# A ranked graph pass in two float32r terms of full width instead of three bf16 terms of half width

## The chip, the core and the metric

The kernel runs on one core of a Trainium2 chip. The core has a matmul engine (TensorE: PE for the matmuls, PEld for its weight loads), VectorE (DVE), ScalarE (ACT), GpSimd (POOL) and SyncE (SP, which issues most DMAs). Each engine works through its own queue in order. SBUF is the working memory; PSUM, eight banks of 128 partitions by 512 float32 numbers, takes the matmul results. The metric is the device time of one execution in microseconds; the median of runs is compared.

## What is computed

Four graph layers over x (3327 nodes by 64 features) and a sparse weighted adjacency matrix, padded here to 3328 by 3328. Every layer is a layernorm and a relu, then the layer's own work, added to x. Layer 0 is two gated cells (GRU), each with one product adj @ (h W). Layer 2 is three products with adj * adj, layer 3 two products with adj. Layer 1 is the one that matters here:

```python
support = input @ weight
mask = (adj != 0).astype(support.dtype)
rank = jnp.cumsum(mask, axis=1)
deg = rank[:, -1:]
k = jnp.minimum(deg, float(MAX_NEIGH))        # 100
pos = rank - (deg - k)
w = mask * jnp.where(pos > 0, DECAY ** (k - pos), 0.0)   # DECAY = 0.5
out = w @ support + bias
```

So the last neighbour of a row has weight 1, the one before it a half, and so on: every weight is an exact power of two that depends on how many neighbours stand behind it. There are eight passes over the adjacency matrix, k = 0 to 7; k = 2 is this "ranked" pass, k = 3, 4, 5 use the squared matrix, the rest the plain one.

## The kernel before

The transposed matrix lies in HBM. A `Tile` is 128 sources (q = 0 to 25) by the two halves of the targets, for one of two groups of target columns: group 0 is chunks 0 and 1 (384 columns each for either half), group 1 is chunks 2 (384) and 3 (512). A unit is (pass k, chunk c, tile t). For every plain or squared unit `propagate` (L579) runs two f32 matmuls, one for each half of the targets; their 64 stationary columns stand in the two halves of the array, so that the two results share one PSUM bank.

`joint(g, k, ...)` (L655) lists the units of two successive passes of one group, with one load of each tile for both: `joint(0, 1)` is k=1 and k=2 of group 0, `joint(1, 2)` is k=2 and k=3 of group 1. The second pass of a pair lags by `later` tiles. `run` (L711) goes through the list of units: it loads tiles ahead into NBUF = 20 buffers, has masks and squares made ahead, calls `expand` (L484) EXPAND = 3 units ahead, and then `propagate`. That order, written out when the program is built, is the order of every engine's queue. Work between passes (`after_1`, `after_2`, ...) runs as tasks: `spend` counts model time, and when a task's time is up its next instructions are put in the queues.

In the ranked pass a tile's 0/1 mask (bf16, made by DVE at L466; its row 127 is replaced by the counts of neighbours behind this tile, by a POOL DMA at L471) is multiplied by the triangular matrix `tri`. Its entries are multiples of 2^7, so the sum in PSUM is 128 times an exponent, and where no edge is, far below zero. ACT (L523, Relu with a bias) or DVE (L521, add and max with 0) turns that sum into an int16, whose bits are those of the bf16 number 2^exponent: `e`. Which engine takes the half s=1 is set by a rule on tile and chunk (L511 to L519); s=0 is always ACT. The features of the pass are split by `in_three` (L912) into three bf16 terms, which add up to the f32 value. A ranked unit is thus, on PE, two triangle products (L510, L307, each a pair of half-width matmuls) and three terms (L607, each a pair). A `SPECIAL` unit at the end of each chunk handles the sources in row 127 of all tiles, with weights `lastw` (L576) and features `lasty` (gathered by POOL DMAs, L928).

PSUM is split in two pools of four banks: sums, and temporaries, though `take` (L316) lends a sums bank when it has been free for longer. After the pass, `after_2` (L961) evacuates the sum, multiplies by the weight matrix (block-diagonal `bd`, two targets halves at once), adds it to x and runs the next layernorm.

Of the kernel before, what the change touches and what calls it, by code (L numbers as in the profile page):

```python
# [11 lines left out]
I16 = mybir.dt.int16  # L12
AF = mybir.ActivationFunctionType
# [31 lines left out]
N, D = 3327, 64  # L45
# [14 lines left out]
TWO27 = float(2 ** 27)  # L60
CAP = 100.0
BITS = (CAP - 128.0) * TWO7

# [10 lines left out]
NBUF = 20  # L74
# [3 lines left out]
EXPAND = 3  # L78
# [5 lines left out]
def chunk_of(b):  # L84
    return next(c for c, (b0, b1) in enumerate(CH[:NC]) if b0 <= b < b1)
# [6 lines left out]
def upper(n):  # L92
    return slice(n * D, (n + 1) * D)
# [3 lines left out]
def kernel(  # L97
# [13 lines left out]
    work = ctx.enter_context(tc.tile_pool(name="work", bufs=4))  # L111
    psum = ctx.enter_context(tc.tile_pool(name="psum", bufs=1, space=bass.MemoryType.PSUM))
# [15 lines left out]
    both = [const.tile([P, 2, (b1 - b0) * P], F32, name=f"both{c}") for c, (b0, b1) in enumerate(CH[:NC])]  # L128
    both += [both[1][:, :, (CH[c][0] - CH[1][0]) * P:(CH[c][1] - CH[1][0]) * P] for c in PARTS]
# [7 lines left out]
    bitsb = const.tile([P, 1], F32, name="bitsb")  # L137
# [4 lines left out]
    lasty = const.tile([P, 2, 3, D], BF16, name="lasty")  # L142
# [95 lines left out]
    def more_constants():  # L238
# [19 lines left out]
        nc.gpsimd.memset(bitsb, BITS)  # L258
        nc.gpsimd.memset(lasty, 0.0)
# [23 lines left out]
        for h in range(2):  # L283
            nc.sync.dma_start(out=bd[upper(h), :, upper(h)], in_=weights[:, WL1:WL3])
            for i in range(2):
                nc.sync.dma_start(out=w3[upper(h), :, i], in_=weights[:, WL3 + (h + i) % 2:NW:2])
# [23 lines left out]
    idle_sums, idle_temps = deque(range(4)), deque(range(4, 8))  # L310
    banks = [psum.tile([P, CWM], F32, name=f"sum{i}") for i in range(4)]
    banks += [psum.tile([P, CWM], F32, name=f"temp{i}") for i in range(4)]

    released = [0] * 8

    def take(sums=False, either=True):  # L316


        either = either and not sums
        pool = idle_sums if sums else idle_temps  # L320
        if either and idle_sums and (not pool or released[idle_sums[0]] < released[pool[0]]):
            pool = idle_sums
        for c in list(tasks):
            if not pool and c not in running:
                advance(c)
        i = pool.popleft()
        return i, banks[i]

    def give(i):
        released[i] = max(released) + 1  # L330
        (idle_sums if i < 4 else idle_temps).append(i)
# [106 lines left out]
    def square(sq, v, turn):  # L438
        if turn % 3 or any(ch in tasks or (2, ch) in sums for ch in range(NC)):
            nc.scalar.activation(sq, v, AF.Square)  # L440
        else:
            nc.vector.tensor_tensor(sq, v, v, ALU.mult)  # L442
# [40 lines left out]

    def expand(k, c, t):  # L484

        if k == COUNT:
            return None
        w = width(c)
        if t is SPECIAL:
            g = c // 2  # L490
            w0 = (CH[c][0] - CH[GROUPS[g][0]][0]) * P
            finish(NC + 1 + g)
            return lastw[g][:, w0:w0 + w].bitcast(BF16)
        if KIND[k] == PLAIN or (KIND[k] == SQUARED and t.in_place):
            return t.view(c)
        if KIND[k] == SQUARED:
            room = Mask(t.w)
            wide = room.view.rearrange("p s w -> p (s w)").bitcast(F32)[:, :2 * w].rearrange("p (s w) -> p s w", s=2)
            square(wide, t.view(c), t.q + c)
            squared[k, c, t] = room  # L500
            return wide
        wide = work.tile([P, 2, CWM], I16, name="e", bufs=4)[:, :, :w]

        mask_pieces(t=t)
        for s in range(2):
            i, ps = take()
            mm(ps[:, :w], tri, t.mask.view[:, s, t.cols(c)])  # L510
            own = chunk_of(t.q % NB) in GROUPS[t.g]  # L511
            busy = any((k - 1, ch) in sums for ch in GROUPS[t.g])
            if t.g == 1 and not own and not relief["squares"]:

                on_vector = s and c == GROUPS[1][1]
            elif relief["pieces"]:
                on_vector = s and (t.q + c) % 4
            else:
                on_vector = s and (own if t.g == 0 and (own or busy) else c == GROUPS[t.g][1] or t.g == 1 and not own)  # L519
            if on_vector:  # L520
                nc.vector.tensor_scalar(wide[:, s], ps[:, :w], BITS, 0.0, op0=ALU.add, op1=ALU.max)  # L521
            else:
                nc.scalar.activation(wide[:, s], ps[:, :w], AF.Relu, bias=bitsb)  # L523
            give(i)
        spend(STREAM_US * w / CWM * 0.5)
        if c == GROUPS[t.g][1]:
            t.mask.free()
        return wide.bitcast(BF16)
# [4 lines left out]
    def count(t, first, last):  # L533
# [3 lines left out]
        for c in GROUPS[t.g]:  # L537
            w = width(c)
            if first:
                counts[c] = take(either=False)  # L540
# [17 lines left out]
    def last_sources(g):  # L558
# [17 lines left out]
        nc.scalar.activation(lastw[g], v, AF.Relu, bias=bitsb)  # L576
        room.free()

    def propagate(k, c, t, rhs, first, last):  # L579
# [4 lines left out]
        if first:  # L584
            sums[k, c] = [take(sums=True) for _ in range(2 if k == 7 and c == PARTS[1] else 1)]
            sums[k, c] = [sums[k, c][0], sums[k, c][-1]]
        acc = sums[k, c]
        if t is SPECIAL:
# [3 lines left out]
            terms = [[lasty[:, h, i, :] for h in range(2)] for i in range(3)]  # L592
            rhs = [rhs, rhs]
        else:
# [4 lines left out]
            terms = [[yk[:, b - CH[cs][0], s, :]] * 2 for yk in (y[k][cs] if KIND[k] == RANKED else [y[k][cs]])]  # L599
            rhs = [rhs[:, h, :] for h in range(2)]  # L600
            if KIND[k] != RANKED:
                t.used()
            if (k, c, t) in squared:
                squared.pop((k, c, t)).free()
        for n, yq in enumerate(terms):
            for h in range(2):
                nc.tensor.matmul(acc[h][1][h * D:(h + 1) * D, :w], yq[h], rhs[h], start=first and n == 0,  # L607
                                 stop=last and n == len(terms) - 1)
        if t is not SPECIAL and t.early and t.mask is None:
            make_mask(t, RANKED)  # L610
        spend(STREAM_US * w / CWM * (0.75 if KIND[k] == RANKED else 1.0))
# [300 lines left out]
    def in_three(h, c):  # L912

        room = both[c].bitcast(BF16).rearrange("p s w -> p (s w)")[:, :blocks(c) * 2 * 3 * D]
        room = room.rearrange("p (b s i d) -> p b s i d", s=2, i=3, d=D)
        terms = [room[:, :, :, i, :] for i in range(3)]
        for i in range(2):
            yield 0.8
            nc.scalar.copy(terms[i], h)
            yield 0.8  # L920
            nc.vector.tensor_tensor(terms[2] if i else h, h, terms[i], ALU.subtract)

# [6 lines left out]
        return terms  # L929
# [18 lines left out]
    def after_1(c, acc):  # L948
# [7 lines left out]
        yield from layernorm_relu(yk, c, TWO27, 1.2 * pace, squares_on_scalar=c in GROUPS[1])  # L956
        y[2][c] = yield from in_three(yk, c)
# [3 lines left out]
    def after_2(c, acc):  # L961
        m = evacuate(acc, c)
        yield 1.4
        v = dense_to_nodes(m, WL1, c)
# [23 lines left out]
    def after_5(c, acc):  # L988
# [8 lines left out]
        yield 8.0  # L997
        yield from transpose_on_vector(yk, c)
# [28 lines left out]
    joint(1, 0, sweep=6, later=4, keep=3, lag=2)  # L1027
# [58 lines left out]
```

## Time and profile before

| what | us |
| --- | --- |
| median of 3 runs | 707.11 (706.21 to 707.22) |
| span of the profiled execution, first to last instruction | 703.7 |
| DVE busy, whole span | 350.1 |
| ACT busy, whole span | 271.8 |
| f32 matmuls of the plain and squared passes (L607), busy | 534.5 |
| bf16 matmuls of the ranked terms (L607), busy | 78.5 |
| triangle matmuls (L307) into the pool of temporaries, busy | 56.8 |
| Relu to int16 on ACT (L523), 145 instructions | 66.0 and 16.6 |
| add and max on DVE (L521), 63 instructions | 38.0 |

The first exponent conversion starts at 204.5 us and the last ranked matmul ends about 338 us. Busy time of PE counts overlapping matmuls once. A group in the profile is a source line with an engine and an operation; L307 is a helper (`mm`) that several callers share.

### The profile page before, as it was taken

The page shows a single profiled execution, that of the slowest core. Times are in us where ns is not written, and L with a number is a line of the kernel's source. Part 1 is how long each engine was busy: PE and PEld are TensorE (multiplying, and loading weights), DVE is VectorE, ACT ScalarE, POOL GpSimd, SP SyncE. Part 2 cuts the span into 40 slices and gives each one's busy share as a digit, 9 for nine tenths or more (in the row PEclk, how much of TensorE's full clock was granted, in tenths as well). Part 3 has the DMA queues.
Part 4 walks back from the last instruction along what each step waited for, and adds up shares of the span by engine and source line. Part 5 has one row for each costly group of instructions (what it writes and reads, how often), then busy time and mean ns, then how long its engine had stood idle before and what let it go on. Part 6 is the DMA issues. An engine that isn't in the chain of part 4 may idle for free.

```text
span 703.7 us, 12628 instructions
## 1 busy us (share of the span) xinstructions
PE 679.8 (97%) x5100; PEld 372.9 (53%) x5100; DVE 350.1 (50%) x746; ACT 271.8 (39%) x422; POOL 80.0 (11%) x114
## 2 busy tenths in 40 slices
PE   1999999999999999999999999999999999999997
PEld 1454666643556787677444444333344444344586
DVE  7556835643997889847523105425271565005101
ACT  1014100122146888888998206832166600000101
POOL 4300000002284233111100000000000000000000
PEclk9999999999999999999999999999999999999999
DMA  9999996089686952683799649973998399927991
GB/s 344 401 385 404 406 405 241 2 314 398 209 279 253 371 177 76 246 297 96 265 390 343 245 151 409 405 276 100 398 366 271 107 391 406 406 81 276 402 403 45
DMA packets 68549, 201.31 MB, mean 286 GB/s; under 512 B 7228, under 2 KB 8228, under 8 KB 68492
## 3 DMA queue, kind: packets, MB, share of 16 engines
q1 hardware_dynamic: 65596, 199.46, 75.9%
q8 instruction: 40, 0.66, 0.4%
q10 hardware_dynamic: 720, 0.85, 0.3%
q0 software_dynamic: 2176, 0.20, 0.2%
q14 instruction: 17, 0.14, 0.1%
HBM read 199.45 MB, written 0.85 MB: 285 GB/s over the span
## 4 chain that ended last, share of the span: by engine, by line
PE 91%; DVE 7%; issue 0%; ACT 0%; DMA 0%; POOL 0%; ACTq 0%; DVEq 0%; POOLq 0%
PE sum L607 77%; PE temp L307 5%; PE temp L542 2%; PE temp L876 2%; PE sum L307 1%; DVE adj L466 1%; PE temp L774 1%; PE sum L876 1%; DVE e L521 1%; DVE st L842 1%; DVE adj L901 1%; DVE t L836 1%; DVE y L841 0%; DVE st L834 0%; DMA xs<-in_x 0%
## 5 line engine op out<-in xcount | busy, mean ns | idle before, releaser
L607 PE MATMUL sum<-adj,y 128*64 128x384 f32 (+3 forms) x3016 | 534.5, 502 | 0.7 <-DVE y L849 0.6
L607 PEld LDWEIGHTS sum<-adj,y 128*64 128x64 f32 x3016 | 243.5, 137 | 237.3 <-issue 212.4
L440 ACT ACTIVATE adj<-adj 128x768 f32<-128x768 f32 (+1 forms) x176 | 144.2, 893 | 45.8 <-PE sum L607 21.9
L466 DVE TENSOR_SCALAR adj<-adj 128x768 bf16<-128x768 f32 (+3 forms) x208 | 114.0, 597 | 39.8 <-PE temp L542 31.8
L824 ACT COPY both<-sum 64x384 f32<-64x384 f32 (+3 forms) x17 | 8.1, 478 | 192.6 <-PE sum L607 191.4
L607 PE MATMUL sum<-e,both 128*64 128x384 bf16 (+1 forms) x624 | 78.5, 339 | 0.5 <-DVE e L521 0.5
L523 ACT ACTIVATE e<-temp,bitsb 128x384 int16<-128x384 f32 (+1 forms) x117 | 66.0, 605 | 15.1 <-PE temp L307 9.9
L825 DVE COPY both<-sum 64x384 f32<-64x384 f32 (+3 forms) x17 | 9.6, 569 | 110.5 <-ACT both L824 110.5
L307 PE MATMUL temp<-adj,tri 128*64 128x384 bf16 (+1 forms) x332 | 56.8, 341 | 0.5 <-DVE e L521 0.2
L442 DVE TENSOR_TENSOR adj<-adj 128x768 f32<-128x768 f32 (+1 forms) x32 | 30.6, 1005 | 52.1 <-DMA adj<-in_adjT 33.4
L845 POOL TENSOR_TENSOR st<-st,mhalf 128x6 f32<-128x6 f32 (+1 forms) x16 | 24.0, 1498 | 283.2 <-DVE st L843 279.5
L607 PEld LDWEIGHTS <-both 128*64 128x64 bf16 x624 | 46.6, 110 | 15.5 <-issue 2.2
L307 PEld LDWEIGHTS <-tri 128*64 128x64 bf16 x416 | 33.5, 110 | 15.3 <-issue 7.1
L521 DVE TENSOR_SCALAR e<-temp 128x384 int16<-128x384 f32 (+1 forms) x49 | 30.1, 617 | 21.1 <-ACT e L523 10.5
L471 POOL DMA_DIRECT2D adj<-totals x52 | 31.5, 607 | 51.2 <-PE temp L307 40.9
L803 DVE STREAM_TRANSPOSE both<-y 32x96 f32<-32x96 f32 (+1 forms) x128 | 35.6, 278 | 2.9
L542 PE MATMUL temp<-adj,behind 128*64 128x384 bf16 x208 | 30.3, 339 | 0.9 <-DVE adj L466 0.7
L819 DVE STREAM_TRANSPOSE y<-t 32x96 f32<-32x96 f32 (+1 forms) x64 | 17.8, 278 | 24.9 <-ACT t L810 24.0
L542 PEld LDWEIGHTS <-behind 128*64 128x64 bf16 x208 | 17.0, 110 | 17.6 <-issue 15.9
L755 DVE COPY t<-sum 128x384 f32<-128x384 f32 x6 | 3.3, 555 | 35.3 <-PE sum L607 35.3
L564 POOL MEMSET adj<- 128x768 f32 (+1 forms) x2 | 1.9, 950 | 145.3 <-PE sum L607 145.3
L523 ACT ACTIVATE e<-sum,bitsb 128x384 int16<-128x384 f32 (+1 forms) x28 | 16.6, 598 | 2.5 <-PE sum L307 2.1
(132 smaller groups left out, 327.8 us busy)
## 6 DMA issues: line engine op xcount, KB each, us to landing
adj<-in_adjT SPq DMA_DIRECT2D x130, 768.0 KB, 8.5
adj<-in_adjT SPq DMA_DIRECT2D x104, 896.0 KB, 12.3
xs<-in_x SPq DMA_DIRECT2D x1, 640.0 KB
adj<-totals POOLq DMA_DIRECT2D x26, 3.0 KB, 5.1
adj<-totals POOLq DMA_DIRECT2D x26, 3.5 KB, 3.0
out<-xs ACTq DMA_DIRECT2D x2, 192.0 KB
out<-xs ACTq DMA_DIRECT2D x1, 256.0 KB
stage<-in_weights SPq DMA_DIRECT2D x2, 112.0 KB, 13.1
```

The lines of the kernel that those rows point to most:

```text
L307: nc.tensor.matmul(out[hs], lhsT[:, hs], rhs, start=start, stop=stop)
L440: nc.scalar.activation(sq, v, AF.Square)
L442: nc.vector.tensor_tensor(sq, v, v, ALU.mult)
L466: nc.vector.tensor_scalar(t.mask.view[:rows, half], t.view()[:rows, half], 0.0, None, op0=ALU.not_equal)
L471: nc.gpsimd.dma_start(out=t.mask.view[P - 1:P], in_=totals[t.g][t.q:t.q + D + 1:D, :])
L521: nc.vector.tensor_scalar(wide[:, s], ps[:, :w], BITS, 0.0, op0=ALU.add, op1=ALU.max)
L523: nc.scalar.activation(wide[:, s], ps[:, :w], AF.Relu, bias=bitsb)
L542: nc.tensor.matmul(counts[c][1][s * D:(s + 1) * D, :w], behind[:, NQ - 1 - t.q:NQ - 1 - t.q + D], t.mask.view[:, s, t.cols(c)], start=firs ...
L607: nc.tensor.matmul(acc[h][1][h * D:(h + 1) * D, :w], yq[h], rhs[h], start=first and n == 0, stop=last and n == len(terms) - 1)
L803: nc.vector.transpose(to[at:at + 32, :, q], h[q * 32:(q + 1) * 32, :, s, f * 32:(f + 1) * 32])
L845: nc.gpsimd.tensor_tensor(st[:, 3, :n], st[:, 2, :n], mhalf[:, :n], ALU.pow)
L876: nc.tensor.matmul(ps[upper(1 - s), :w], cells[:, cell, s, g, :], both[c][:, s], start=True, stop=True)
```

## The change

- The features are split in two float32r terms (`in_two`): ACT's copy rounds to float32r, DVE's subtraction gives the rest. The two stand side by side as 128 stationary columns. Each target half needs a bank of its own, so a ranked sum holds two banks for each chunk, and one matmul for each half replaces three pairs. `after_2` evacuates two banks and adds the two terms' rows by way of the weight matrix, which for this layer stands twice one above the other.
- The weights `e` are float32r. ACT computes exp(ln2/128 * sum + bias), which rounds to the exact power of two when it is written. On DVE the conversion to int16 stays, and a second instruction multiplies the bits, read as bf16, by a constant and writes float32r. The rule is now: half s=1 of a group 0 tile goes to DVE if the chunk is 1 or q is odd, all else goes to ACT. The special unit gets one such multiplication.
- The triangle product is one matmul of 128 stationary columns for each half.
- While ranked sums are open, three of four squares of k=3 go to DVE; before, all went to ACT then.
- One pool of eight PSUM banks; NBUF 19 instead of 20, EXPAND 2 instead of 3, keep=2 instead of 3 in `joint(1, 0)`. `both` buffers come from a pool and are allocated anew for the terms and again after pass 5. The scale is 2^38 instead of 2^27.

```diff
-NBUF = 20
+NBUF = 19
-EXPAND = 3
+EXPAND = 2
...
-    idle_sums, idle_temps = deque(range(4)), deque(range(4, 8))
...
+    idle = deque(range(8))
+    banks = [psum.tile([P, CWM], F32, name=f"bank{i}") for i in range(8)]
...
     def square(sq, v, turn):
-        if turn % 3 or any(ch in tasks or (2, ch) in sums for ch in range(NC)):
+        ranked = any((2, ch) in sums for ch in range(NC))
+        if turn % 4 == 0 if ranked else turn % 3 or any(ch in tasks for ch in range(NC)):
             nc.scalar.activation(sq, v, AF.Square)
...
+    def weight():
+        return work.tile([P, CWM], F32R, name="e", bufs=2 * (EXPAND + 1))
+
     def expand(k, c, t):
...
-            return lastw[g][:, w0:w0 + w].bitcast(BF16)
+            e = weight()
+            nc.vector.tensor_scalar(e[:, :w], lastw[g][:, w0:w0 + w].bitcast(BF16), DROP, None, op0=ALU.mult)
+            return e, e
...
         for s in range(2):
             i, ps = take()
-            mm(ps[:, :w], tri, t.mask.view[:, s, t.cols(c)])
...
+            nc.tensor.matmul(ps[:, :w], tri, t.mask.view[:, s, t.cols(c)], start=True, stop=True)
+            e = weight()
+            if s and t.g == 0 and (c == GROUPS[0][1] or t.q % 2):
+                bits = work.tile([P, CWM], I16, name="bits", bufs=2)
+                nc.vector.tensor_scalar(bits[:, :w], ps[:, :w], BITS, 0.0, op0=ALU.add, op1=ALU.max)
+                nc.vector.tensor_scalar(e[:, :w], bits[:, :w].bitcast(BF16), DROP, None, op0=ALU.mult)
             else:
-                on_vector = s and (own if t.g == 0 and (own or busy) else c == GROUPS[t.g][1] or t.g == 1 and not own)
...
-                nc.scalar.activation(wide[:, s], ps[:, :w], AF.Relu, bias=bitsb)
+                nc.scalar.activation(e[:, :w], ps[:, :w], AF.Exp, bias=bitsb[:, 1:2], scale=LN2 / TWO7)
             give(i)
...
-            sums[k, c] = [take(sums=True) for _ in range(2 if k == 7 and c == PARTS[1] else 1)]
+            sums[k, c] = [take() for _ in range(2 if KIND[k] == RANKED or k == 7 and c == PARTS[1] else 1)]
...
+        if KIND[k] == RANKED:
+            for h in range(2):
+                nc.tensor.matmul(acc[h][1][:, :w], terms[h], rhs[h][:, :w], start=first, stop=last)
...
-        spend(STREAM_US * w / CWM * (0.75 if KIND[k] == RANKED else 1.0))
+        spend(STREAM_US * w / CWM * (0.5 if KIND[k] == RANKED else 1.0))
...
+    def in_two(h, c):
+
+        room = stacked.tile([P, blocks(c), 2, P], F32R, name=f"both{c}")
+        yield 0.8
+        nc.scalar.copy(room[:, :, :, :D], h)
+        yield 0.8
+        nc.vector.tensor_tensor(room[:, :, :, D:], h, room[:, :, :, :D].bitcast(F32), ALU.subtract)
+        yield 1.5
...
     def after_2(c, acc):
-        m = evacuate(acc, c)
+        w = width(c)
+        m = [work.tile([P, CWM], F32, name="t2")[:, :w] for _ in range(2)]
+        nc.scalar.copy(m[0], acc[0][1][:, :w])
+        nc.vector.tensor_copy(m[1], acc[1][1][:, :w])
+        for n in range(2):
+            give(acc[n][0])
         yield 1.4
-        v = dense_to_nodes(m, WL1, c)
+        i, ps = take()
+        v = i, view(ps, c)
+        for b in range(blocks(c)):
+            for s in range(2):
+                for n in range(2):
+                    nc.tensor.matmul(v[1][upper(n), b, upper(s)], m[s][:, b * P + n * D:b * P + (n + 1) * D],
+                                     bd[:, 0, upper(0)], start=True, stop=True)
...
-    joint(1, 0, sweep=6, later=4, keep=3, lag=2)
+    joint(1, 0, sweep=6, later=4, keep=2, lag=2)
```

## The prediction

> **What bounds the kernel now.** First the page's header, its engine line and its chain of work:
>
> ```profile
> span 703.7 us, 12628 instructions
> PE 679.8 (97%) x5100; PEld 372.9 (53%) x5100; DVE 350.1 (50%) x746; ACT 271.8 (39%) x422; POOL 80.0 (11%) x114
> PE 91%; DVE 7%; issue 0%; ACT 0%; DMA 0%; POOL 0%; ACTq 0%; DVEq 0%; POOLq 0%
> ```
>
> The matmul engine (PE) ends the program, but the averages hide stages. The change touches one stage, the ranked pass, so next comes the table of engine busy time by stretch: 200 to 219 us (two ranked tiles among f32 units), 219 to 248 (group 0 against group 1's sources, beside the GRU and layernorm of group 0), 248 to 269.3 (group 0 against its own sources), and group 1 in the last three:
>
> ```profile
> 200.00:219.00 19.00, 19.00 (x144) 10.90 (x142) 16.95 (x32) 10.47 (x20) 17.80 (x20) 1.00 0.58 195
> 219.00:248.00 29.00, 27.48 (x333) 20.27 (x331) 24.19 (x52) 22.91 (x48) 5.84 (x9) 1.00 0.98 374
> 248.00:269.30 21.30, 21.30 (x267) 18.41 (x264) 18.57 (x37) 15.98 (x31) 4.94 (x9) 1.00 0.40 132
> 269.30:284.50 15.20, 13.98 (x147) 9.77 (x145) 14.91 (x30) 13.24 (x24) 6.80 (x9) 1.00 0.37 121
> 284.50:316.50 32.00, 32.00 (x256) 22.79 (x254) 19.43 (x35) 27.66 (x42) 3.76 (x7) 1.00 0.80 279
> 316.50:338.00 21.50, 21.50 (x235) 15.92 (x233) 16.14 (x29) 19.18 (x33) 3.27 (x6) 1.00 0.43 134
> ```
>
> Columns: stretch, length, then busy PE, PEld, DVE, ACT, POOL, the clock (full), DMA. PE is full nearly everywhere, but VectorE (DVE) is at 24.2 of 29.0, 18.6 of 21.3 and 14.9 of 15.2, and ScalarE (ACT) at 16 to 28 just behind. There is little room on either. Third, the timeline of one ranked unit (a chunk times a source tile) in the steady part:
>
> ```profile
> 250.09 0.36 PE L307 MATMUL temp<-adj,tri 128*64 128x384 bf16 x2
> 250.25 0.36 PE L307 MATMUL sum<-adj,tri 128*64 128x384 bf16 x2
> 250.41 0.68 PE L607 MATMUL sum<-e,both 128*64 128x384 bf16 x6
> 250.53 0.58 ACT L523 ACTIVATE e<-temp,bitsb 128x384 int16<-128x384 f32 x1 [0.23 <-DVE e L521]
> 250.70 0.56 DVE L521 TENSOR_SCALAR e<-sum 128x384 int16<-128x384 f32 x1 [0.26 <-PE sum L307]
> ```
>
> Five pairs of half-width matmuls, each pair 0.1625 us from start to start (250.09, 250.25, 250.41): 0.81 us a unit at 384 columns. At 512 columns the pairs stand 0.215 apart (269.10 to 269.32): 1.08.
>
> Last, the groups kept apart by shape, for prices:
>
> ```profile
> L523 ACT ACTIVATE e<-temp,bitsb 128x384 int16<-128x384 f32 x94 | 50.6, 585 | 13.5 <-PE temp L307 9.2 <-ACT adj L440 3.1 <-DVE e L521 0.9
> L521 DVE TENSOR_SCALAR e<-temp 128x384 int16<-128x384 f32 x26 | 14.3, 554 | 5.1 <-PE temp L307 2.6 <-ACT adj L440 1.2 <-issue 0.6
> L466 DVE TENSOR_SCALAR adj<-adj 128x768 bf16<-128x768 f32 x52 | 27.8, 582 | 16.0 <-PE temp L542 15.9
> L881 ACT ACT_TABLE_LOAD x1 | 1.3, 1283 | 0.0
> ```
>
> Queued back to back, ACT starts L523 every 0.467 us (235.29, 235.75, 236.21) and its 512-wide form every 0.575 (0.69 less the same overlap).
>
> **Matmuls.** Triangle: two full-width matmuls instead of two half-width pairs, the same streaming time. Feature terms: two full-width float32r matmuls instead of three bf16 pairs. No row shows float32r or a 128-column weight load. The nearest rows are the bf16 pair (0.1625 us at 384 columns) and the f32 pair (0.644: five units from 199.60 to 202.82). Less than the bf16 row is excluded, since as many columns stream. I take the bf16 row: the new matmul is one record over the moving tile if it is a single pass, as bf16 is, while the f32 rows hold two records a matmul. Then a unit takes four pair times instead of five: 78 units of 384 columns, 26 of 512 and the four special units (three and one) save 81 x 0.1625 + 27 x 0.215 = 19 us of PE work. At two pair times a matmul a unit takes six, and the change costs 19 us; at the f32 row, four each, it takes ten: +95. Weight loads are hidden now (64 columns 110 ns, behind 162); 128 columns at twice that, 220 ns, would expose 58 ns on each of 4 x 104 matmuls, 24 us. I take zero, since loads of the next pair run while this one streams.
>
> The Trainium skill's FP8 and Floating Point Precision page, section TensorE Precision Notes, tells true FP32 (four passes) from a reduced FP32 that is read as four bytes and truncated. No run here shows the latter, and no term uses it.
>
> **ACT.** Exponential for Relu, same shape and bias. Nearest rows at 384 columns: L523 itself, 585 ns, the sigmoid L881 580 and the tanh L897 615; I take L523. Halves on ACT: in group 0 2.5 of 4 a tile (now 65 of 98 from 219 to 269), in group 1 all 4 (now 70 of 101). A group 1 tile costs ACT 2 x 0.467 + 2 x 0.575 = 2.08 us, where PE needs 4 x (0.1625 + 0.215) = 1.51 and takes 1.89 now. So in pure ranked stretches of group 1 **ACT becomes the bound**. Worse, two sums for each chunk take four banks and the k=3 sums two, which leaves two for the triangle: ACT 0.585, release about 0.1, triangle 0.33, 0.05 to ACT gives 1.05 for two halves' bank, about 0.48 a half; 0.61 at 512. I use 2.19 a tile.
>
> New table loads: exponentials and sigmoids alternate between 204 and 224 us, in my reading five extra switches. By the row, 1.283 each, 6.4 us, three of them before 219 where ACT idles 8.5 us, two in 219 to 248. I count nothing for PE, up to 3 us if exposed. ScalarE: Activation LUTs, section What ACT_TABLE_LOAD costs, speaks harder against the change: a switch also drains, 2.66 us in all, which would make 13.3 us of the five; the two loads of this trace show 1.283 and an idle of 0.0 before the second, so the drain isn't seen.
>
> **DVE.** A half on DVE is now two instructions: L521 (0.555), then bits (bf16 in SBUF) to float32r. Nearest rows for the second: the in-SBUF L905, 352 ns at 384 columns, and L521's own 555; below, the small 162 to 172 ns rows. L466 does 768 columns from SBUF in the time of 384 from PSUM, so I take 0.352. Dependent, they make 0.59 + 0.36 less 0.08 overlap with the next, 0.86 us (0.7 to 1.06). Group 0 has 39 such halves, 18 each in 219-248 and 248-269. Two chunks lose one subtract of in_three each (1.1 us), and an ACT cast. Three in four squares of k=3 go to DVE while the ranked sums live: some 17 of 22, about 1.05 each, 17 us, in stretches where L521 leaves (20 us): even.
>
> **Sum by stretch.**
> 200-219: four units save 0.65; table loads take it; 0.
> 219-248: DVE 24.19 - 7.28 (L521) - 1.1 + 18 x 0.86 = 31.3, PE only 27.5 - 3.9 = 23.6. PE waits for each half, and the GRU and layernorm work sits in the same DVE queue. 31.3 plus 1 of waiting for the GRU: 32.3 for 29.0, **+3.3**.
> 248-269.3: DVE 18.57 - 10.32 + 15.5 + 0.7 (special weights) = 24.5 for 21.3, **+3.2**. Mask pieces (6.4 us) stand in that queue.
> 269.3-284.5, seven tiles of group 1: ACT 13.24 - 9.86 - 3.52 + 14.6 + 0.9 + 0.5 = 15.9 for 15.2; **+1** with banks.
> 284.5-316.5, nine tiles with eleven k=3 tiles between: PE falls by 9 x 0.378 = 3.4, ACT hides in the f32 matmuls, but the second triangle waits some 0.27 a cycle for a bank: **-1.5**.
> 316.5-338: five tiles at 2.19 for 1.89, then six units at 0.96 for 0.81 and six at 1.2 for 1.08, special units -0.4: **+2.5** (ACT alone says 23.5 for 21.5).
> In all +8.5: 703.7 becomes 712.2 of span. The page gives the profiled execution's span alone; the median of the runs shown, 707.11, stands 3.4 us over it, which I take as what lies around it: 715.6.
>
> Nothing for: one buffer fewer and keep=2 (PE waits 0.9 us for adjacency DMA in all; cover is the prefetch, up to +2 if it thins); two more SP weight loads and wider lasty DMAs on POOL's queue (landing long before use); the merged bank pool elsewhere; the second evacuation in after_2, on the other engine; its 64-column dense matmuls (0.89 for 24 records against 0.85 for 12).
>
> **Rivals.** *PE keeps the pace* (0.25). The masks, residuals and layernorm work that I count against PE in 219-269 may slide behind the halves PE needs; then these stretches are PE's: 23.6 + 1.5 and 17.1, -3.9 and -4.2. With group 1 at bare ACT speed (+0.7, -3.4, +2.0) the sum is -8.8: 698. It decides once a pair costs DVE under about 0.6, or the queue isn't in order of need. For it: 12 us of DVE idle later in 284-316. Against: 24.2 of 29.0 busy already.
> *Float32r isn't one pass, or its weights show* (0.10). Two bf16 times per matmul: PE's 19 us saving becomes a loss of 19: 726. Exposed loads, +24 on PE's reduced work, come to 712 to 726. It shows as a spacing over 0.17 at 384 columns.
> *It does not matter* (0.07): gains and losses cancel, 706 to 708.5; PE's wait replaced by equal DVE and ACT waits.
> Forecast, a modest loss as DVE then ACT become the bound (0.58): 710 to 722; with the unknown pair price (0.7: -5.8; 1.06: +7), banks and table loads.
>
> Below 698 lies about half of the first rival's lower tail, above 727 the dearer matmul; the range 698 to 727 holds eight in ten. Faster by over 0.2% (about what a measurement of this kernel can tell) 0.27, within 0.2% 0.06, slower 0.67. The losing cases' own range is 710 to 727.
>
> **What will show it.** Float32r spacing near 0.162; PE idle of 8 us or more in 219-269 with DVE (the second tensor_scalar) as releaser; DVE above 90% there; five more table loads; in the pure stretch of group 1, ACT solid, a tile each 2.1 to 2.2 us. Wrong if PE stays full through 219-338, or if the second tensor_scalar takes under 0.2 us.

## The result and the profile after

The changed kernel takes 736.21 us (736.05 to 736.85) beside 706.85 us for the kernel before on the same chip: a ratio of 1.0426 with a 95% interval of 1.0411 to 1.0442, 29.4 us lost. The prediction said slower, by 8.5 us, and ended its range at 727.

The page of the changed kernel, its header, its engine line and its chain of work:

```profile
span 734.9 us, 11444 instructions
PE 691.6 (94%) x4510; PEld 334.6 (46%) x4512; DVE 367.2 (50%) x783; ACT 277.6 (38%) x429; POOL 79.5 (11%) x115
PE 78%; DVE 13%; ACT 5%; DMA 1%; issue 1%; SPq 0%; POOL 0%; ACTq 0%; DVEq 0%; POOLq 0%
```

There are 590 matmuls fewer, and yet PE is busy 12 us longer (691.6 for 679.8). The chain now runs 13% through VectorE and 5% through ScalarE, where it had 7% and 0%. Neither engine's total says why: each has only 6 to 17 us more work.

Next the stretches, cut so that each holds nearly the same work in both kernels: at the copy that evacuates the last k=1 sum of group 1, at the first special unit of group 0, at the first k=3 unit, at the end of the stretch that mixes k=3 with ranked tiles, and at the end of the ranked pass. In the kernel before they last 19.17, 43.11, 22.18, 32.42 and 21.02 us, with PE idle 0, 1.5, 1.2, 0 and 0 us of them. The second one of before (columns: stretch, length, then busy PE, PEld, DVE, ACT, POOL, the granted clock, DMA):

```profile
219.17:262.28 43.11, 41.59 (x507) 32.50 (x504) 36.16 (x74) 34.09 (x69) 10.41 (x17) 1.00 0.85 314
```

All five of the changed kernel:

```profile
200.00:226.38 26.38, 22.98 (x115) 8.75 (x112) 18.25 (x38) 11.47 (x17) 16.99 (x22) 0.94 0.70 250
226.38:277.87 51.49, 43.50 (x256) 24.70 (x255) 46.37 (x106) 35.95 (x65) 9.93 (x15) 0.93 0.62 213
277.87:302.98 25.11, 21.53 (x131) 11.86 (x130) 24.22 (x52) 20.25 (x39) 8.76 (x12) 1.00 0.13 39
302.98:339.10 36.12, 35.96 (x155) 11.71 (x156) 24.58 (x34) 25.14 (x42) 3.90 (x6) 1.00 0.77 277
339.10:363.70 24.60, 21.64 (x113) 11.93 (x112) 12.25 (x22) 23.88 (x44) 3.23 (x7) 1.00 0.30 101
```

The loss by stretch is 7.2, 8.4, 2.9, 3.7 and 3.6 us; after the ranked pass come 5.4 more (371.2 us for 365.8). No stretch alone explains it. In the second, DVE has 46.4 of 51.5 us, for 36.2 of 43.1, and is the busiest engine; in the fourth PE is full and still slower; in the fifth ACT is solid, 23.9 of 24.6. The clock column falls below full only in the first two; PE also stands idle for 3.6 us of the third and 3.0 us of the fifth, at a full clock.

Four readings of single rows. The new instructions, shapes apart (line, operation, out and in, count, then busy us and mean ns):

```profile
L530 ACT ACTIVATE e<-bank,bitsb 128x384 fp32r<-128x384 f32 x117 | 63.3, 585 | 30.7 <-PE bank L523 29.1
L528 DVE TENSOR_SCALAR e<-bits 128x384 fp32r<-128x384 bf16 x39 | 14.6, 373 | 2.0
L609 PEld LDWEIGHTS bank<-e,both 128*128 128x128 f32 x208 | 37.2, 191 | 37.8 <-issue 23.4 <-DVE e L528 6.2 <-ACT e L530 2.8
L523 PEld LDWEIGHTS <-tri 128*128 128x128 bf16 x208 | 12.9, 99 | 28.6 <-issue 25.1 <-DVE adj L478 1.3 <-DMA lasty<-both 0.2
```

The exponential costs what Relu cost (585 ns), and the second VectorE instruction 373 ns (0.352 was taken). A 128-column load takes 99 ns in bf16 and 191 in float32r.

The timeline of a pure ranked unit of group 0 (no matmul of another pass stands between), which answers to the one shown of before:

```profile
254.69 0.50 PE L523 MATMUL bank<-adj,tri 128*128 128x384 bf16 x2
254.89 0.65 PE L609 MATMUL bank<-e,both 128*128 128x384 f32 x2
...
255.38 0.50 PE L523 MATMUL bank<-adj,tri 128*128 128x384 bf16 x2
```

One unit takes 0.69 us (254.69 to 255.38) for 0.81 before. So **float32r is a single pass**: four matmuls at 0.172 us each, beside 0.1625 of a bf16 pair; two passes would have made 0.98. But just ahead of this unit, in the same stretch, the second triangle had waited for a bank that VectorE had not yet emptied:

```profile
254.01 0.32 PE L523 MATMUL bank<-adj,tri 128*128 128x384 bf16 x1 [0.53 <-DVE bits L527]
```

And in the pure stretch of group 1 a tile repeats every 2.26 us (346.30 to 348.56), where PE has 1.55 us of work (0.69, and four times 0.215 at 512 columns). The second triangle at 384 columns waits for a bank in every tile:

```profile
346.30 0.32 PE L523 MATMUL bank<-adj,tri 128*128 128x384 bf16 x1 [0.25 <-ACT e L530]
...
348.56 0.32 PE L523 MATMUL bank<-adj,tri 128*128 128x384 bf16 x1 [0.25 <-ACT e L530]
```

Last, part of the 5.4 us behind the ranked pass lies in pass 5, where the chain stands for 4.7 us on a transfer of the adjacency. PE itself is idle for 2.7 us of that time (from 579.7 to 582.35, until the square L454 that the transfer feeds), and the clock shows 0.76 in the 5 us from 580:

```profile
576.54 4.68 DMA adj<-in_adjT
```

### The profile page after: what moved, and what is told of

The parts are those of the page before. It is cut to its first block, busy times and chain, and to the rows that moved or that the text cites. A ratio compares the mean times of both kernels' runs of the same rounds, so it can differ in the third digit from the quotient of the medians.

```text
span 734.9 us, 11444 instructions
## 1 busy us (share of the span) xinstructions
PE 691.6 (94%) x4510; PEld 334.6 (46%) x4512; DVE 367.2 (50%) x783; ACT 277.6 (38%) x429; POOL 79.5 (11%) x115
## 4 chain that ended last, share of the span: by engine, by line
PE 78%; DVE 13%; ACT 5%; DMA 1%; issue 1%; SPq 0%; POOL 0%; ACTq 0%; DVEq 0%; POOLq 0%
PE bank L615 66%; ACT e L530 4%; DVE adj L478 3%; PE bank L883 2%; PE bank L550 2%; PE bank L523 2%; DVE bits L527 2%; PE bank L609 2%; DVE e L528 1%; PE bank L781 1%; PE bank L324 1%; DVE t L843 1%; DVE st L841 1%; DVE adj L908 1%; DMA adj<-in_adjT 1%
## 5 line engine op out<-in xcount | busy, mean ns | idle before, releaser
L615 PE MATMUL bank<-adj,y 128*64 128x384 f32 (+3 forms) x3016 | 536.2, 505 | 3.8 <-DVE adj L454 2.7
L615 PEld LDWEIGHTS bank<-adj,y 128*64 128x64 f32 x3016 | 226.9, 138 | 260.9 <-issue 226.6
L530 ACT ACTIVATE e<-bank,bitsb 128x384 fp32r<-128x384 f32 (+1 forms) x169 | 94.3, 622 | 32.6 <-PE bank L523 31.0
L454 DVE TENSOR_TENSOR adj<-adj 128x768 f32<-128x768 f32 (+1 forms) x52 | 51.6, 1029 | 59.2 <-DMA adj<-in_adjT 47.3
L609 PE MATMUL bank<-e,both 128*128 128x384 f32 (+1 forms) x208 | 71.7, 427 | 3.9 <-DVE e L528 2.4
L523 PE MATMUL bank<-adj,tri 128*128 128x384 bf16 (+1 forms) x206 | 62.1, 351 | 11.4 <-ACT e L530 5.0
L609 PEld LDWEIGHTS bank<-e,both 128*128 128x128 f32 x208 | 37.2, 191 | 37.8 <-issue 23.4
L550 PE MATMUL bank<-adj,behind 128*64 128x384 bf16 x208 | 30.3, 340 | 0.9 <-DVE adj L478 0.7
L527 DVE TENSOR_SCALAR bits<-bank 128x384 int16<-128x384 f32 x39 | 21.5, 551 | 8.9 <-PE bank L523 8.8
L883 PE MATMUL bank<-both,cells 128*64 128x384 f32 (+1 forms) x112 | 23.5, 532 | 0.0
```

Source lines behind the costliest of these rows:

```text
L523: nc.tensor.matmul(ps[:, :w], tri, t.mask.view[:, s, t.cols(c)], start=True, stop=True)
L527: nc.vector.tensor_scalar(bits[:, :w], ps[:, :w], BITS, 0.0, op0=ALU.add, op1=ALU.max)
L530: nc.scalar.activation(e[:, :w], ps[:, :w], AF.Exp, bias=bitsb[:, 1:2], scale=LN2 / TWO7)
L550: nc.tensor.matmul(counts[c][1][s * D:(s + 1) * D, :w], behind[:, NQ - 1 - t.q:NQ - 1 - t.q + D], t.mask.view[:, s, t.cols(c)], start=firs ...
L609: nc.tensor.matmul(acc[h][1][:, :w], terms[h], rhs[h][:, :w], start=first, stop=last)
L615: nc.tensor.matmul(acc[h][1][h * D:(h + 1) * D, :w], terms[h], rhs[:, h, :], start=first, stop=last)
```

## Experiments

Theories: **conversions** (the second VectorE instruction, and ScalarE with all of group 1's halves), **layout** (loads of 128 columns, and of another width than the one before, show), **banks** (two sums a chunk leave the triangle two free banks), **buffers**, **table loads**. The kernel before ran beside all of them, at 706.1 to 706.9. Seven of the twelve runs make a ladder from the kernel before to the changed one, each rung one part of the change. Medians in us; the columns between are times read from each trace: the copy that ends group 1's k=1, the start of group 0's first special unit, the end of the ranked pass, the span.

| kernel | median | step | copy | special | end of pass | span |
|---|---|---|---|---|---|---|
| before | 706.1 | | 219.2 | 262.3 | 337.9 | 703.7 |
| two half-width bf16 terms, one pool (e12) | 699.03 | -7.1 | 219.4 | 257.6 | 329.9 | 696.3 |
| + a second bank held per chunk (e9) | 708.76 | +9.7 | 220.7 | 261.5 | 340.6 | 706.9 |
| + full width (e7) | 712.43 | +3.7 | 220.6 | 263.0 | 343.6 | 710.6 |
| + 19 buffers, two ahead (e10) | 717.69 | +5.3 | 223.1 | 263.5 | 345.3 | 715.2 |
| + float32r (e8) | 721.35 | +3.7 | 224.0 | 265.1 | 352.1 | 722.0 |
| + its split of halves and squares (e4) | 724.95 | +3.6 | 225.0 | 268.3 | 351.8 | 723.1 |
| + second VectorE instruction (e5) | 736.40 | +11.4 | 225.7 | 277.2 | 363.0 | 734.2 |
| + exponential (the changed kernel) | 736.21 | -0.2 | 226.4 | 277.9 | 363.7 | 734.9 |

The medians have some 1 us of spread, e8 more (719.44 and 720.64 at a mean clock of 0.999, 722.05 and 723.89 at 0.994), so the two rungs beside e8 are known to about 2 us each; their sum, 7.3, is firmer. The trace of e8 is that of its slowest run, so its times in the table stand some 2.5 us late. Each rung holds for this order of steps: a part taken alone can cost more (the triangle in e2) or less.

**e1, buffers alone.** `NBUF = 20` to `19` and `keep=3` to `2` in the kernel before.

> The kernel before with 19 adjacency buffers and keep=2, nothing else changed. The changed kernel's trace has one wait of 4.7 us for an adjacency DMA at 576 us (pass 5 of group 0), far from the ranked pass, which the kernel before hasn't. Theory A, the lost buffer makes that wait: 706.9 + 4.6 = 711.5, with the same wait in pass 5. Theory B, it is a late effect of the ranked pass (transfers shifted against the work): 707, no wait.

709.46 (708.37 to 712.62), ratio 1.0053 [1.0034, 1.0071]: a cost, but not at the late wait. The trace is that of its slowest run (712.62). There the chain of waits holds an adjacency transfer of 7.36 us at 209, and the time behind the ranked pass is that of the kernel before (365.8 us).

**e2, the triangle alone at full width.** In the kernel before:

```diff
-            mm(ps[:, :w], tri, t.mask.view[:, s, t.cols(c)])
+            nc.tensor.matmul(ps[:, :w], tri, t.mask.view[:, s, t.cols(c)], start=True, stop=True)
```

> The kernel before with the triangle product as one matmul of 128 stationary columns for each half instead of a pair of 64; the terms stay bf16 pairs of 64. The streaming time on PE is the same, no engine gets other work. Theory L (layout): changing between full-width and half-width stationary operands leaves a weight load uncovered. In the changed kernel's stretch with k=3 units each change shows 0.10 to 0.18 us over the streaming time. Here each of 104 ranked units has two changes, some 0.1 to 0.15 each: +20 to +30 where PE is full, so 722 to 735. Theory C (conversions on DVE and ACT are the whole cost): 707.

723.99, ratio 1.0248 [1.0231, 1.0265]: **17.7 us for a change that streams the same columns.** A unit of group 0:

```profile
256.88 0.34 PE L510 MATMUL sum<-adj,tri 128*128 128x384 bf16 x1
...
257.31 0.30 PEld L607 LDWEIGHTS <-both 128*64 128x64 bf16 x6 [0.32 <-issue]
257.31 0.68 PE L607 MATMUL sum<-e,both 128*64 128x384 bf16 x6
...
257.92 0.34 PE L510 MATMUL temp<-adj,tri 128*128 128x384 bf16 x1
```

It takes 1.04 us for 0.81. Two triangles take 0.43 (256.88 to 257.31) for 0.325, and three pairs of terms 0.61 (257.31 to 257.92) for 0.49: each passage from 128 stationary columns to 64 or back shows about 0.1 us. The load of the new width starts only with its first matmul (both at 257.31), where in the kernel before the loads run some 0.16 us ahead (249.93 for a matmul at 250.09). Why it is not issued earlier stays open: the trace gives no releaser but the issue. Two passages in each of 104 units would make some 21 us by these 0.1, beside the 17.7 measured. So a mix of widths is dear; the changed kernel has full width in both matmuls of a ranked unit and meets the mix only beside k=1 and k=3 matmuls.

**e3, one term fewer.** In the kernel before, the third bf16 term is neither loaded nor summed (the features then carry two terms' digits):

```diff
-... for yk in (y[k][cs] if KIND[k] == RANKED else [y[k][cs]])]
+... for yk in (y[k][cs][:2] if KIND[k] == RANKED else [y[k][cs]])]
```

> The kernel before with two of its three bf16 terms (the third is left out, so the features count with 16 bits). PE loses the same 19 us of streaming that the change was to save, with the conversions, the layout and the banks as before. Theory G1, PE's saving is there to be had when nothing else is added: 706.9 - 19 + stalls of a few us, 690 to 695. Theory G2, the conversions were already next behind PE (DVE 24.2 of 29.0 and 18.6 of 21.3 us busy): 697 to 704.

699.25 (698.06 to 701.0), ratio 0.9903 [0.9883, 0.9923]. This takes out just the 19 us of PE work that the prediction credits, and besides only the planner's price of a unit: only 7.1 come back. From 269.3 to 284.5 VectorE is busy 15.06 of 15.2 us and PE 11.3, and up to 322.88 PE waits 2.7 us for a mask row that a DMA brings behind VectorE's mask piece (L466, then L471). The triangle's group of e3, with what ended its idle time:

```profile
L307 PE MATMUL temp<-adj,tri 128*64 128x384 bf16 (+1 forms) x332 | 52.7, 344 | 6.1 <-DMA adj<-totals 2.7 <-DVE e L521 1.3 <-DVE xs L854 1.3
```

**e4, both conversions made cheap.** In the changed kernel, Relu for the exponential, and the VectorE half written to the weight tile by its first instruction. Both change the values of the weights.

```diff
-                nc.vector.tensor_scalar(bits[:, :w], ps[:, :w], BITS, 0.0, op0=ALU.add, op1=ALU.max)
-                nc.vector.tensor_scalar(e[:, :w], bits[:, :w].bitcast(BF16), DROP, None, op0=ALU.mult)
+                nc.vector.tensor_scalar(e[:, :w], ps[:, :w], BITS, 0.0, op0=ALU.add, op1=ALU.max)
...
-                nc.scalar.activation(e[:, :w], ps[:, :w], AF.Exp, bias=bitsb[:, 1:2], scale=LN2 / TWO7)
+                nc.scalar.activation(e[:, :w], ps[:, :w], AF.Relu, bias=bitsb[:, 1:2], scale=LN2 / TWO7)
```

> The changed kernel with two costs taken out: Relu in place of the exponential (no table loads; the weights are wrong) and DVE's half written straight from PSUM as float32r in one instruction (the second instruction is left out; wrong weights too). Layout, banks, number of ACT conversions and buffers stay. Theory C: the DVE pair (39 x 0.36 = 14 us on a full DVE), six table loads of 1.28 and the stalls and slow clock that follow them made most of the loss: 714 to 720. Theory L: the layout makes most: 727 or more.

724.95, ratio 1.0266 [1.0251, 1.0281]: 11.3 us below the changed kernel, between the two theories. More than half of the loss is not in the price of a conversion.

**e5 and e6, the two halves of e4.** e5 has the Relu line alone, e6 the VectorE lines alone.

> The changed kernel with Relu in place of Exp on ScalarE (its weights are then wrong; the float32r terms, the pair of VectorE instructions, the banks and the buffers stay). It splits the 11.3 us that the cheap conversions gave (724.95 against 736.21). Theory T, the table switches between exponential and sigmoid (six loads of 1.283 us on ScalarE) stop PE between 204 and 228 and the granted clock falls after it (0.66 to 0.89 in stretches of 5 us, about 5 us of PE): 726 to 730. Theory P, the second VectorE instruction is what costs: 733 to 736.

> The changed kernel with Exp kept and the second VectorE instruction of a half left out: the first one writes its result to the weight tile directly (wrong weights for those halves). Theory P, VectorE is what ends last from 239 to 290, and 39 instructions of 0.373 us go: 726 to 730, about 6 to 10 below 736.2. Theory T (table switches and the clock): 733 to 736. If both this and the Relu kernel give their part, the two gains should add up to about 11.

e5: 736.40 (734.61 to 737.24), ratio 1.0419 [1.0399, 1.0439], the changed kernel again. e6: 725.55, ratio 1.0268 [1.0253, 1.0283], nearly all of e4's gain. **The table switches cost nothing that these runs can tell (736.21 with them for 736.40 without, 725.55 for e4's 724.95); the second VectorE instruction costs 11.** My theory T, which I had read from PE's waits at 223 to 225 beside the loads, falls: the waits and the lower clock are there without the loads as well. The changed kernel and e6 have three loads at the sigmoid and three at the exponential, 1283 ns each, where e5 has one at the sigmoid; the times go with the second VectorE instruction, not with the loads. What the second instruction adds on VectorE, 39 times 0.373 us, is 14.6 us, and most of it is paid between the copy and the first special unit: 51.5 us in the changed kernel, 43.5 in e6 (225.21 to 268.70), 43.1 before. The stretch in e6:

```profile
225.21:268.70 43.49, 38.14 (x255) 23.26 (x254) 36.52 (x77) 35.04 (x65) 9.57 (x15) 1.00 0.73 252
```

VectorE has 36.5 us there for 46.4, and the clock is full for 0.93. So of the 8.0 us in this stretch up to some 3.6 (an estimate, 0.07 of 51.5) go with the clock: the windows of 5 us at 225, 230 and 245 show 0.77, 0.89 and 0.69. These dips come behind waits of PE, but not every wait brings one: e6 has PE busy 3.45 of the 5 us from 230, and a full clock there.

**e7, full width in bf16.** The kernel before with two bf16 terms side by side in 128 columns, a full-width triangle, two banks a chunk and one pool; its conversions, rules and 20 buffers.

```diff
+            for h in range(2):
+                nc.tensor.matmul(acc[h][1][:, :w], terms[h], rhs[h][:, :w], start=first, stop=last)
...
+        room = stacked.tile([P, blocks(c), 2, 2 * P], BF16, name=f"both{c}")[:, :, :, :P]
```

> The kernel before with its first two bf16 feature terms side by side in 128 stationary columns, a full-width triangle, two banks a chunk and one pool of banks; its int16 weights, its Relu, its split of the halves over ScalarE and VectorE and its 20 buffers stay. It computes what the half-width kernel with two terms computes (699.25), with the same count of columns streamed in half as many instructions. Theory L, each change between 64 and 128 stationary columns shows 0.1 to 0.18 us of weight load (it occurs with the other passes' matmuls between the ranked ones), and two sums a chunk leave few banks: 706 to 712. Theory C, conversions on VectorE and ScalarE are all of the loss: 698 to 701.

712.43 (710.8 to 713.11), ratio 1.0080 [1.0064, 1.0095]: 13 us above the same sums at half width, with no float32r, no exponential and no second instruction in it. It does not say whether layout or banks did it; e9 does.

**e8, cheap conversions and the old split.** e4 with the rule of the kernel before for which half goes to VectorE and which squares to ScalarE.

> The changed kernel with Relu, one VectorE instruction a half, and the rule of the kernel before for which half goes to VectorE and which squares go to ScalarE (so ScalarE does 70 instead of 101 halves of group 1, and VectorE the others); wrong weights. Against the cheap conversions alone (724.95): theory S, ScalarE alone sets the pace of group 1's pure ranked tiles (2.26 us a tile for 1.89): 716 to 720. If the two free banks set the pace there, whichever engine converts: 723 to 726. What is then left over 699.25, the two-term kernel, is layout, banks and one buffer fewer.

721.35 (719.44 to 723.89), ratio 1.0211 [1.0185, 1.0237], 3.6 below e4, less than expected. The gain is not where theory S puts it: a pure tile of group 1 takes 2.16 us (332.33 to 334.49) with VectorE helping, 2.26 with ScalarE alone, and PE's work is 1.55. Something else holds it there:

```profile
303.16 0.60 PE L522 MATMUL bank<-adj,tri 128*128 128x512 bf16 x2
...
332.33 0.85 PE L522 MATMUL bank<-adj,tri 128*128 128x512 bf16 x2
...
334.49 0.85 PE L522 MATMUL bank<-adj,tri 128*128 128x512 bf16 x2
```

Two triangles at 512 columns span 0.85 here, where 0.60 is their span without a wait, at 303.16 among k=3 matmuls of the same kernel. ScalarE's busy column in the fifth stretch of the changed kernel (23.9 of 24.6) therefore overstates its part. Which of the two rules gave the 3.6 was not tried.

**e9 and e12, banks alone.** Both sum two bf16 terms as half-width pairs, with one pool and the rest of the changed kernel's code around it, but with the conversions, the rules and the 20 buffers of the kernel before. e9 also takes a second bank for each ranked chunk, which lies unused until the chunk's sum is evacuated; e12 does not.

```diff
-            sums[k, c] = [take() for _ in range(2 if k == 7 and c == PARTS[1] else 1)]
+            sums[k, c] = [take() for _ in range(2 if KIND[k] == RANKED or k == 7 and c == PARTS[1] else 1)]
+            if KIND[k] == RANKED:
+                held[c] = sums[k, c].pop()
```

> Two bf16 terms as half-width pairs (as in the two-term kernel, 699.25) with the bank use of the changed kernel: one pool, and a second bank is taken for each ranked chunk and lies unused until the chunk's sum is evacuated, so the triangle has two free banks in group 1. It computes the same as the two-term kernel and the full-width bf16 kernel (712.43). Theory B, the banks are what the full width loses in the pure tiles of group 1 (2.15 us a tile there for 1.51 of PE work): 705 to 709, and a pure tile takes 2.1 to 2.2. Theory L, it is the layout: 699 to 702, and the tile takes 1.5 to 1.9.

> Two bf16 terms as half-width pairs with one bank a chunk, like the two-term kernel, but with the one pool of banks and the rest of the changed kernel's code around it; the one with held banks less the held banks. It should be the two-term kernel again if the single pool, the new place for the terms and the order that follows are neutral: 698 to 701. Over 703 would put part of the loss on the single pool.

e12: 699.03, ratio 0.9895 [0.9879, 0.9912], so the single pool is free. e9: 708.76, ratio 1.0033 [1.0022, 1.0044]: **an unused bank a chunk costs 9.7 us**, theory B. A pure stretch in e12, then in e9:

```profile
312.07 0.52 PE L323 MATMUL bank<-adj,tri 128*64 128x384 bf16 x4
...
313.58 0.52 PE L323 MATMUL bank<-adj,tri 128*64 128x384 bf16 x4
```

```profile
328.67 0.82 PE L323 MATMUL bank<-adj,tri 128*64 128x384 bf16 x4
...
329.75 0.82 PE L323 MATMUL bank<-adj,tri 128*64 128x384 bf16 x4
```

In e12 a tile of one 384 and one 512 chunk takes 1.51 us (312.07 to 313.58) without a gap, which is the PE time of the prediction to the hundredth. In e9 a single 384 unit takes 1.08 (328.67 to 329.75) for 0.65, and a tile of both chunks 2.33 (323.09 to 325.42). Triangle, conversion, release, triangle is a loop through two banks, whatever the triangle's width: from 225 us to the end of the pass PE waits 2.6 us in e9 for a bank that ScalarE's conversion empties (L533), and 0.4 in e12, counting only the waits that the trace names. In the mixed stretch e9's triangle also stands 0.33 us a cycle. In e7 it stands 0.24 (299.43 to 300.10, for 0.43 of streaming), and the cycle's two changes of width show 0.09 and 0.15; so the two costs partly hide one another, and full width, with the second evacuation that goes with it, adds only 3.7.

**e10, the planning.** e7 with 19 buffers, two expansions ahead and keep=2.

> The full-width bf16 kernel (712.43) with the planning of the changed kernel: 19 adjacency buffers for 20, two expansions ahead for three, keep=2 for 3. What is then left to the kernel with float32r and cheap conversions (721.35) is float32r itself and its longer weight loads. Theory F, float32r loads show (3.78 for 3.51 us in each mixed cycle with k=3, about 11 of them, and a little in pure tiles) and make most of the 8.9 us: 712 to 715. Theory N, the buffers do (as in the kernel before with 19 buffers, +3.1, and the adjacency wait of 4.7 us late in the program belongs to them): 716 to 720.

717.69, ratio 1.0159 [1.0144, 1.0174]: 5.3 us, the range of theory N; which of the three settings makes it was not tried. By the ladder 2.5 come before the copy and 2.9 behind the ranked pass (369.9 us for 367.0). The late wait is there, 4.77 us of adjacency transfer at 558 (PE idle 2.8), though not in e1, where the same count of buffers meets the old layout with three expansions ahead. The changed kernel's tail is 1.3 longer still (371.2); that was not followed.

The rest of the way to e8, 3.7 us, is float32r with its longer loads, and the multiplications of the special units that come with it. A pure unit takes 0.69 us, for 0.65 in e10 (255.42 to 256.07). The mixed cycle of k=3 and ranked units takes 3.02 us in e3, 3.51 in e7 (297.11 to 300.62), 3.53 in e10 (297.72 to 301.25), 3.70 in e8 (301.93 to 305.63) and 3.78 in the changed kernel:

```profile
310.03 0.50 PE L523 MATMUL bank<-adj,tri 128*128 128x384 bf16 x2
310.46 0.87 PE L615 MATMUL bank<-adj,y 128*64 128x384 f32 x4
311.26 0.69 PE L523 MATMUL bank<-adj,tri 128*128 128x512 bf16 x2
311.87 1.08 PE L615 MATMUL bank<-adj,y 128*64 128x512 f32 x4
312.88 1.09 PE L609 MATMUL bank<-e,both 128*128 128x384 f32 x4
313.81 0.50 PE L523 MATMUL bank<-adj,tri 128*128 128x384 bf16 x2
```

No row names another engine as what it waits for. From start to start two triangles take 0.43 and 0.61 (0.325 and 0.43 in half-width pairs) and the f32 matmuls 0.80 and 1.01 (0.645 and 0.86): 0.10 to 0.18 more at each of the four changes of width. The wider triangles take only 0.54 in e8 and 0.53 in e10, so a change of width itself shows 0.10 to 0.16. The float32r row is followed by a triangle of its own width, and takes 0.93 where 0.755 is streaming. With bf16 terms, in e10, it takes 0.76:

```profile
300.49 0.93 PE L613 MATMUL bank<-e,both 128*128 128x384 bf16 x4
301.25 0.49 PE L521 MATMUL bank<-adj,tri 128*128 128x384 bf16 x2
```

So these 0.17 are float32r's own. By an estimate of ten such cycles in the 36 us of the stretch they make 1.7 of the 3.7.

**e11, all of group 1 on ScalarE.** e3 with the changed kernel's rule for group 1, an attempt at a better version.

```diff
-                on_vector = s and c == GROUPS[1][1]
+                on_vector = False
```

> The two-term kernel (699.25) with all halves of group 1 on ScalarE, as the changed kernel has them; nothing else. In the two-term kernel the mask pieces on VectorE are late at 265 to 277 and at 317 to 322 (PE waits 3.4 us for a row that is copied in by DMA after a piece). If VectorE's queue makes them late, this frees it and gives 694 to 698; if ScalarE's four halves a tile (2.1 us for 1.51 of PE) bind instead, as in the changed kernel's pure stretch, 700 to 704.

706.79, ratio 1.0015 [1.0004, 1.0027], 7.5 above e3 and past what I expected. From 280 to 312 ScalarE is full and VectorE has 9 us:

```profile
280.00:312.00 32.00, 29.96 (x202) 18.24 (x199) 8.98 (x16) 32.00 (x51) 4.19 (x6) 1.00 0.77 258
```

The k=3 squares on ScalarE (L440) queue there with the halves, 22.9 of the 32.0 us. That moved halves need moved squares, as the changed kernel has them, is a reading of this and was not tried. The two-term kernels e3 and e12 are faster than both kernels of this case; they leave out the third term.

## Why the prediction was wrong, by its own steps

The ladder adds to 30.1 us (its first rung stands on a run of before 0.75 us lower than the one beside the changed kernel). The prediction's +8.5 failed in four terms and undersized a fifth; the rest held.

1. **"Save 81 x 0.1625 + 27 x 0.215 = 19 us of PE work."** True of the streaming: e12's pure tile is 1.51 us as worked out, and float32r at the bf16 row was off by 0.04 a unit. But e3 and e12 show what that work is worth by itself, 7.1. The prediction did cap group 0 by VectorE, and so credited less than 19; it did not look at which DMA and mask piece come next in group 1.
2. **Banks: "the second triangle waits some 0.27 a cycle for a bank: -1.5".** The loop of 1.05 us for two halves was right (1.08 in e9, 0.24 to 0.33 of waiting a cycle in the traces). But half of it is 0.53, not the 0.48 that the sum went on with; with 0.53 the pure tile comes to 2.28, beside the 2.26 measured. And it was spent only where k=3 ran and inside ScalarE's 2.19. Group 0, with the same two sums a chunk, was given none, though the triangle there waits for "bits" 0.5 to 0.8 us. Measured by itself it is +9.7 against the two-term kernel.
3. **Weight loads: "I take zero, since loads of the next pair run while this one streams."** Right within a run of bf16 of the same width (0.65 a unit in e10), wrong at each passage between 64 and 128 columns, where the load does not run ahead: +3.7 for layout after the banks, and 17.7 alone in e2. Float32r, whose loads take 191 ns, adds another 3.7 (0.69 a unit, and 0.17 a mixed cycle). The trace before had no such passage, and the 24 us from a doubled load stayed with a rival of 0.10.
4. **"Nothing for: one buffer fewer and keep=2 ... up to +2 if it thins."** +3.1 in e1; +5.3 in e10, which also looks two units ahead for three. In e10 2.9 of it come far behind the pass, where a transfer is late (558 in e10, 576 in the changed kernel).

**The second VectorE instruction** was mechanism right, size off. 0.86 us a pair was near (0.55 + 0.373 with an overlap). The sum 219 to 269 said +6.5; the instruction alone gave 10.7 (e6) to 11.4 (e5 to e4), of which about 4, an estimate, go with the granted clock (the mean clock of 0.989 is 8.1 us short of full over 734.9, e6's 0.994 is 4.3 short over 723.5), a term that the prediction lacked: it held the clock at 1.00 while it predicted PE idle. The prediction also named the second instruction as what PE would wait for. From 225 to 364 us PE waits 4.0 us for the first (L527), which empties a bank, and 0.7 for the second (L528): the longer queue is felt as a bank that comes free late.

**The split of halves and squares**, ScalarE's +1 and +2.5, stands beside 3.6 on the ladder (e8 to e4), which is known to about 2 us and does not contradict it.

**Right:** slower; VectorE then ScalarE as the engines that end last, though with the banks beside ScalarE (2.16 us a tile in e8, with VectorE's help); 2.26 us a pure tile for 2.19; the stretch of seven tiles near even, by the prediction's own cut (group 0's last special unit to the first k=3 unit: 0.75 us for +1); table loads at nothing (e5). The Trainium skill's page ScalarE: Activation LUTs, section What ACT_TABLE_LOAD costs, would have made 13.3 us of five switches, an estimate from its figure; the run without them is within 0.2 us of the run with them.

**Rivals.** PE keeping the pace fails by the second stretch, 43.5 busy of 51.5. "Float32r isn't one pass, or its weights show" fails in its first half and holds in its second, as one part among several. That it does not matter is out.

## What to carry over

Price the released work by taking it out alone before crediting it: 19 us of PE time were worth 7 here, since VectorE's queue and a DMA stood close behind. A change of shape brings its costs with it where the engines' busy times do not show them: banks that set a loop's length, a stationary width that differs from the neighbours', one buffer less far downstream. And add up instructions on an in-order engine's queue with what their waiting does to the clock.

## What the runs showed of the hardware

Going between 64 and 128 stationary columns showed 0.10 to 0.16 us each time, in bf16 alone as well (e2, 17.7 us in all): the load of the new width starts only with its first matmul. Bf16 loads of one width hide fully behind 0.16 us of streaming (four matmuls of 128 columns in 0.65 us, e10). Float32r streams 384 columns in about 0.17 us (four matmuls, two of them float32r, in 0.69). A load of 128 bf16 columns takes 99 ns, less than the 110 of 64, and one of float32r 191; the Trainium skill's page TensorE: Matmul & The Clock Gate, section Weight-path perf modes, has a fast load for just 128 columns of a type other than FP32, and the bf16 rows agree with it. Five more table loads of 1.283 us changed the time by no more than 0.6 us (e5, and e6 beside e4). The granted clock took values between 0.55 (e1) and 0.98 (e5) in windows of 5 us behind gaps in PE's work, in kernels with and without the exponential's table loads, with 8 us of clock lost in the changed kernel (an estimate from its mean, 0.989) for under 1 before. Gaps alone do not bring it about: e9 has PE busy 3.40 of the 5 us from 230, and a full clock from 190 to 270. What sets off such a dip, and how long it lasts, was not tried.
